# The last 3 of 39 expert blocks of a decoder kernel, put in a conditional block

## The chip, the cores and the metric

One core of one Trainium2 chip. The metric is the device time of one execution in microseconds, the median of three runs.

## The reference, cut to what matters

A decoder of two layers over 8 x 256 = 2048 tokens of width 512, in float32. Layer 0: differential attention, a long convolution with the context, then a mixture of 8 experts, of which each token takes two. Layer 1: self-attention, cross-attention, attention with one routed head. Each of the six parts ends in a residual sum and a layer norm. The expert part is what the change touches:

```python
logits = h @ router_w.T
probs = jax.nn.softmax(logits.astype(jnp.float32), axis=-1)
vals, idx = lax.top_k(probs, TOP_K)            # TOP_K = 2
vals = vals / vals.sum(axis=-1, keepdims=True)
combine = combine.at[jnp.arange(T)[:, None], idx].add(vals)
...
def step(acc, per_expert):
    gup, dp, cw = per_expert
    gate, up = jnp.split(h @ gup.T, 2, axis=-1)
    y = jax.nn.silu(gate) * up @ dp.T
    return (acc + cw[:, None].astype(acc.dtype) * y, None)
```

Two of 8 experts per token make 4096 pairs of a token and an expert. How many fall on which expert is known only when the logits are.

## The kernel before, in words

The stages run one after another on the core. The expert stage overlaps with the end of the convolution and stands directly ahead of self-attention.

**Sending tokens to experts.** `router` computes the logits in two halves of the tokens. Each token row, normalized, is written to `xd` (L761) and, by indirect DMAs on POOL (`send`, L825), to `xs` in DRAM, where every expert has a region of ROWS = 2176 rows; `slots` holds the row of each pair. The tokens of an expert lie there without gaps.

**The table of blocks.** Work is cut into blocks of 128 rows of one expert. `block_table` counts how many blocks each expert needs (`nb`), sums these up along the experts (`end`), and finds for each block number its expert (`i_ex`) and its first row (`i_row`). It runs twice: after the first half of the tokens it lists NE = 9 blocks that are already full; after the second half it lists the other NB - NE = 30. NB = 39 is the most that any routing can need (4096/128 + 7). Where fewer are needed, the remaining numbers get the last expert and rows without tokens, and are computed all the same.

**A block** (`blocks`, from L942) has these steps:
- `load` reads its expert number into a register of TensorE (L955) and its row into one of SP (L962), and SP loads its rows, `first_h<-xs` (L970), 256 KB, into one of four buffers, three blocks ahead;
- `turn` transposes the rows (pt, L188 and L217);
- `gate_up` makes the gate and up products pg and pu (L194), 8 matmuls, and silu on ScalarE and DVE (L1013 to L1015);
- `down` transposes the result (pt_m, L1023), copies it to hT (L1025, L1026), makes the down product po_m (L1032), copies it to y_m (L141 on DVE, L139 or L1041 on ScalarE), and SP stores it to `ys` at the same row (L1044). The row is in a register, so each store of `ys` waits for the one ahead.

For the 9 early blocks the order on TensorE, DVE and ScalarE is written out by hand, between token tiles of the second half. For the other 30, L1080 to L1088, a scheduler sets it by priorities; it lets four downs fall behind, which end the stage in two pairs. During block 18 `meanwhile` starts the loads of self-attention's weights.

**After the blocks.** `combine(t)` (L1090) loads x[t] from `xd` (SP, L1097), gathers the two expert rows of each token from `ys` (POOL, L1099, one indirect DMA per expert choice), and adds them with their weights (DVE, L1108). Layer norm follows: statistics on DVE (L168, L169), the inverse root on POOL (L163, L164), the normalization on DVE (L177). Self-attention works on groups of four tiles; its first group needs t = 0 to 3, and begins with transposes of x (pt, L217) and the products ps_f (L205).

Of the kernel before, what the change touches and what calls it, by code (L numbers as in the profile page):

```python
# [24 lines left out]
P = 128  # L25
B, S, D = 8, 256, 512
# [13 lines left out]
E, FF = 8, 352  # L40
FCH = [(0, 128), (128, 128), (256, 96)]
KPAD = 128 + D
NB = 2 * B * S // P + E - 1
ROWS = B * S + P
PH = NT // 2
NE = (PH * 2 * P - E * (P - 1) - 1) // P + 1
# [3 lines left out]
def decoder_kernel(ctx: ExitStack, tc: tile.TileContext, a: dict, out: bass.AP):  # L50
    nc = tc.nc
# [10 lines left out]
    rt = ctx.enter_context(tc.tile_pool(name="m_rt", bufs=1))  # L62
# [52 lines left out]
    xd = dram.tile([NT, P, D], F32, tag="xd", name="xd")  # L115
    xs = dram.tile([E * ROWS, D], F32, tag="xs", name="xs")
    ys = dram.tile([E * ROWS, D], F32, tag="ys", name="ys")
    ctx_d = dram.tile([P, KB, B * S], F32, tag="ctx_d", name="ctx_d")
# [16 lines left out]
    def evacuate(dst, src):  # L135

        flip[0] ^= 1
        if flip[0]:
            nc.scalar.copy(dst, src)  # L139
        else:  # L140
            nc.vector.tensor_copy(dst, src)  # L141
# [42 lines left out]
    def transpose(psum, dst, src):  # L184

        pt = psum.tile([P, KB, P], F32, tag="tr", name="pt")
        for k in range(KB):
            nc.tensor.transpose(pt[:, k, :], src[:, k * P : (k + 1) * P], ident)  # L188
        evacuate(dst, pt)
# [23 lines left out]
    def turned(pools, dst, src, tag="mm"):  # L213

        pt = pools.tile([P, KB, P], F32, tag=tag, name="pt")
        for k in range(KB):
            nc.tensor.transpose(pt[:, k, :], src[:, k * P : (k + 1) * P], ident)  # L217
        nc.scalar.copy(dst, pt)  # L218
# [436 lines left out]
    def experts(rt):  # L655
# [7 lines left out]
        tables = {}  # L663
# [30 lines left out]
        def clear_slots(pool):  # L694
# [3 lines left out]
            for e in range(E):  # L698
                for region in (xs, ys):
                    nc.sync.dma_start(  # L700
                        out=region[e * ROWS : (e + 1) * ROWS, :].rearrange(
                            "(p r) d -> p r d", p=P
                        ),
                        in_=zero.unsqueeze(1).broadcast_to([P, ROWS // P, D]),
                    )
# [6 lines left out]
        def router(work, rows_late):  # L712
# [15 lines left out]
                base,  # L728
                pattern=[[ROWS, E]],
                base=0,  # L730
# [123 lines left out]
        def block_table(ps_t, counts, half):  # L854
# [3 lines left out]
            def t8(name):  # L858
                return rt.tile([P, E], F32, tag=name, name=name)
# [4 lines left out]
            full = rt.tile([P, NT], F32, tag="full", name="full")  # L864
            blk = rt.tile([P, NB], F32, tag="blk", name="blk")
            for row, step in ((full, P), (blk, 1)):
# [23 lines left out]
            end = t8("end")  # L890
# [6 lines left out]
            nc.vector.tensor_tensor(first, end, nb, ALU.subtract)  # L897
            count = NB - NE if half else NE
            shape = [P, count, E]
            blk = blk[:, :count]  # L900
            bb = blk.unsqueeze(2).broadcast_to(shape)
            c = rt.tile([P, NB, E], F32, tag="c_b", name="c_b")[:, :count]
            nc.vector.tensor_tensor(c, end.unsqueeze(1).broadcast_to(shape), bb, ALU.is_le)
            ex = rt.tile([P, NB], F32, tag="ex", name="ex")[:, :count]
            nc.vector.tensor_reduce(ex, c, AX.X, ALU.add)
# [3 lines left out]
            nc.vector.tensor_tensor(c, c, first.unsqueeze(1).broadcast_to(shape), ALU.mult)  # L909
            row = rt.tile([P, NB], F32, tag="row", name="row_b")[:, :count]  # L910
            nc.vector.tensor_reduce(row, c, AX.X, ALU.max)
            nc.vector.tensor_tensor(row, blk, row, ALU.subtract)
            if half == 0:

                done = tables["done"] = t8("done")
                nc.vector.tensor_scalar(done, first, -1.0, float(NE), ALU.mult, ALU.add)
                nc.vector.tensor_scalar(done, done, 0.0, None, ALU.max)
                nc.vector.tensor_tensor(done, done, nb, ALU.min)
            else:

                nc.vector.scalar_tensor_tensor(
                    c,
                    idx.unsqueeze(1).broadcast_to(shape),
                    float(E),
                    ex.unsqueeze(2).broadcast_to(shape),
                    ALU.add,
                    ALU.is_equal,
                )
                nc.vector.tensor_tensor(
                    c, c, tables["done"].unsqueeze(1).broadcast_to(shape), ALU.mult  # L930
                )
                more = rt.tile([P, NB], F32, tag="more", name="more")[:, :count]
                nc.vector.tensor_reduce(more, c, AX.X, ALU.add)
                nc.vector.tensor_tensor(row, row, more, ALU.add)
            nc.vector.tensor_scalar(row, row, float(NT), float(P), ALU.min, ALU.mult)
            nc.vector.scalar_tensor_tensor(row, ex, float(ROWS), row, ALU.mult, ALU.add)
            for name, src in (("ex", ex), ("row", row)):
# [4 lines left out]
        def blocks(ps_t, buffers, late_tokens, meanwhile):  # L942


            with ExitStack() as st:
# [3 lines left out]
                xb, behind = {}, []  # L949
# [44 lines left out]
                def turn(b):  # L994
                    xT[b] = work.tile([P, KB, P], F32, tag="xT", name="xT_b")
                    if b < NE:
                        turned(ps_t, xT[b], xb[b][2], "tr")
                    else:
                        transpose(ps_t, xT[b], xb[b][2])

                def gate_up(b):
                    e, row, _ = xb.pop(b)
                    x_b = xT.pop(b)
                    pg = psum.tile([P, FF], F32, tag="g", name="pg")
                    pu = psum.tile([P, FF], F32, tag="u", name="pu")
                    for i, ps in enumerate((pg, pu)):
                        project(
                            ps,
                            lambda k: x_b[:, k, :],
                            lambda k: gu[k][i][:, bass.ds(e, 1), :],  # L1010
                        )
                    h = work.tile([P, FF], F32, tag="h", name="h_b", bufs=4)
                    nc.scalar.activation(h, pg, AF.Sigmoid)  # L1013
                    nc.vector.tensor_tensor(h, h, pg, ALU.mult)  # L1014
                    nc.vector.tensor_tensor(h, h, pu, ALU.mult)  # L1015
                    behind.append((b, e, row, h))

                def down(then=lambda: None):

                    b, e, row, h = behind.pop(0)  # L1020
                    pt = ps_t.tile([P, 3, P], F32, tag="tr", name="pt_m")
                    for i, (f0, m) in enumerate(FCH):
                        nc.tensor.transpose(pt[:m, i, :], h[:, f0 : f0 + m], ident)  # L1023
                    hT = work.tile([P, 3, P], F32, tag="hT", name="hT")
                    nc.scalar.copy(hT[:, 0:2, :], pt[:, 0:2, :])  # L1025
                    (nc.scalar.copy if b < NE else nc.vector.tensor_copy)(  # L1026
                        hT[:96, 2, :], pt[:96, 2, :]
                    )
                    then()
                    po = psum.tile([P, D], F32, tag="o", name="po_m")  # L1030
                    for i, (_, m) in enumerate(FCH):
                        nc.tensor.matmul(  # L1032
                            po,
                            lhsT=hT[:m, i, :],
                            rhs=dn[i][:m, bass.ds(e, 1), :],
                            start=(i == 0),
                            stop=(i == len(FCH) - 1),
                        )
                    y = work.tile([P, D], F32, tag="y", name="y_m")
                    if b < NE:  # L1040
                        nc.scalar.copy(y, po)  # L1041
                    else:
                        evacuate(y, po)
                    return nc.sync.dma_start(out=ys[bass.ds(row, P), :], in_=y).ins.name  # L1044
# [32 lines left out]
                        gate_up(b)  # L1077
                        down(lambda: turn(b + 1))
                load(NE + 2)
                for b in range(NE, NB):  # L1080
                    if b + 3 < NB:
                        load(b + 3)
                    gate_up(b)
                    stored = down(lambda: b + 1 < NB and turn(b + 1))
                    if b == NE + 9:
                        meanwhile(stored)
                while behind:
                    down()  # L1088

        def combine(t, buffers):  # L1090

# [21 lines left out]
            return load, add, lambda: norm[0]()  # L1113

        return clear_slots, load_experts, load_gu_last, router, blocks, combine, wide


# [578 lines left out]
    clear_slots, load_experts, load_gu_last, router, blocks, combine, wide = experts(rt)  # L1696
    diff_attention()
    with ExitStack() as st_self:


        half = B * P * KB
# [108 lines left out]
```

## Time and profile before

| what | value |
|---|---|
| median of three runs | 2341.53 us (2339.19 to 2346.2) |
| profiled execution, own time | 2344.37 us |
| its span | 2342.5 us |
| mean granted TensorE clock | 0.971 |
| expert blocks, first pg to last y_m | from 840.4 to 1195.7 us |
| first product ps_f of self-attention | 1223.41 us |
| one ys store, issue to landing, median | 2.0 us |
| one x<-xd load, issue to landing, median | 4.4 us |

All times in the text are microseconds from the start of the span of this profiled execution. PE is TensorE, DVE VectorE, ACT ScalarE, POOL GpSimd, SP the engine that issues most DMAs; PEld is TensorE's weight load, which overlaps its matmuls. A line such as L1032 is a line of the kernel before. In the chain of waits each piece has a start, a length and what ran or was waited for; it is followed back from the last instruction of the execution, so that what is not in it did not set the end. In a list by stretch, each engine has its busy time and, in brackets, its number of instructions.

### The profile page before, as it was taken

The page shows a single profiled execution, that of the slowest core. Times are in us where ns is not written, and L with a number is a line of the kernel's source. Part 1 is how long each engine was busy: PE and PEld are TensorE (multiplying, and loading weights), DVE is VectorE, ACT ScalarE, POOL GpSimd, SP SyncE. Part 2 cuts the span into 40 slices and gives each one's busy share as a digit, 9 for nine tenths or more (in the row PEclk, how much of TensorE's full clock was granted, in tenths as well). Part 3 has the DMA queues.
Part 4 walks back from the last instruction along what each step waited for, and adds up shares of the span by engine and source line. Part 5 has one row for each costly group of instructions (what it writes and reads, how often), then busy time and mean ns, then how long its engine had stood idle before and what let it go on. Part 6 is the DMA issues. An engine that isn't in the chain of part 4 may idle for free.

```text
span 2342.5 us, 35493 instructions
## 1 busy us (share of the span) xinstructions
PE 2170.8 (93%) x15151; PEld 1176.5 (50%) x15151; DVE 1202.4 (51%) x1858; ACT 428.9 (18%) x616; POOL 660.0 (28%) x768
## 2 busy tenths in 40 slices
PE   7799989879998998999959999998999999999996
PEld 4455555544453464555534454444545545555543
DVE  3566666657888962222224556452212213467767
ACT  1223233320010021111112222221101110122212
POOL 0344544456556622000022324230000000022223
PEclk9999999999999998999979999999999999999998
DMA  6899302306024143131140112003001000000000
GB/s 243 330 407 407 143 11 69 98 1 219 28 84 141 32 158 121 61 135 63 50 151 19 46 37 64 1 1 126 19 18 36 1 0 1 1 7 14 10 19 28
DMA packets 108715, 199.10 MB, mean 85 GB/s; under 512 B 7056, under 2 KB 26640, under 8 KB 108560
## 3 DMA queue, kind: packets, MB, share of 16 engines
q1 hardware_dynamic: 103440, 180.06, 21.7%
q0 software_dynamic: 5120, 16.78, 2.2%
q8 instruction: 121, 1.98, 0.3%
q14 instruction: 34, 0.28, 0.0%
HBM read 94.32 MB, written 112.98 MB: 88 GB/s over the span
## 4 chain that ended last, share of the span: by engine, by line
PE 72%; DVE 9%; POOL 8%; DMA 3%; ACT 3%; issue 2%; SPq 1%; another core or an unknown queue 0%; ACTq 0%; POOLq 0%; DVEq 0%
PE ps_y L194 9%; PE ps_f L205 8%; PE ps_t L205 7%; PE ps_f L194 5%; PE po_m L1032 5%; PE pg L194 4%; PE ps_o L205 4%; PE pu L194 4%; PE ps_k L1235 3%; PE ps_q L1181 3%; PE ps_t L194 2%; PE po_x L194 2%; PE ps_o L194 2%; PE ps_pv L1288 2%; POOL pT L1263 2%; POOL pT L1253 2%
## 5 line engine op out<-in xcount | busy, mean ns | idle before, releaser
L1188 DVE TENSOR_REDUCE neg<-ps_q 128x12 f32<-128x1536 f32 x128 | 224.9, 1757 | 342.5 <-PE ps_q L1181 341.7
L194 PE MATMUL ps_y<-kv,wt 128*128 128x512 f32 x640 | 282.4, 600 | 5.7 <-POOL kv L562 3.8
L1253 POOL TENSOR_SCALAR_AFFINE_SELECT pT<-pT 128x1024 f32<-128x1024 f32 x128 | 140.3, 1097 | 513.2 <-ACT pT L1252 443.4
L1252 ACT ACTIVATE pT<-ps_k 128x1536 f32<-128x1536 f32 x128 | 185.8, 1452 | 537.4 <-PE ps_k L1244 515.6
L1296 DVE RECIPROCAL rsum<-ps_pv 128x256 f32<-128x256 f32 x128 | 224.1, 1751 | 40.5 <-PE ps_pv L1288 39.7
L194 PEld LDWEIGHTS ps_y<-kv,wt 128*128 128x128 f32 x640 | 120.9, 192 | 155.7 <-issue 137.0
L163 POOL TENSOR_SCALAR rstd<-bn_mv 128x1 f32<-128x1 f32 x80 | 17.0, 213 | 560.5 <-DVE bn_mv L169 556.5
L1263 POOL TENSOR_TENSOR pT<-pT 128x512 f32<-128x512 f32 x112 | 142.4, 1271 | 9.4
L1032 PE MATMUL po_m<-dn,hT 128*128 (+1 forms) x234 | 113.0, 621 | 12.0 <-ACT hT L1025 10.5
L194 PE MATMUL ps_f<-xT,w_l1x 128*128 128x512 f32 x256 | 120.7, 615 | 3.3 <-ACT qT L1460 2.1
L205 PE MATMUL ps_f<-xT,w_l1a 128*128 128x512 f32 x256 | 119.7, 611 | 3.0 <-ACT xT L218 3.0
L205 PE MATMUL ps_t<-w_l1f,xT 128*128 128x512 f32 x256 | 120.1, 607 | 0.3 <-DVE sel L1627 0.3
L1099 POOL DMA_INDIRECT w_l1x<-ys,slots x32 | 32.6, 1018 | 307.6 <-DMA ys<-y_m 299.7
L1288 PE MATMUL ps_pv<-pT,ones_v 128*32 128x256 f32 (+1 forms) x1152 | 86.0, 381 | 12.7 <-POOL pT L1263 10.6
L600 DVE TENSOR_REDUCE yc<-z 128x64 f32<-128x512 f32 x128 | 86.1, 674 | 6.2 <-POOL w_l1a L601 5.8
L1171 PEld LDWEIGHTS <-ident_b 128*128 128x128 bf16 x512 | 50.4, 99 | 75.4 <-issue 71.6
L1171 PE MATMUL ps_q<-hide_b,ident_b 128*128 128x256 bf16 x512 | 77.7, 275 | 9.7 <-ACT pT L1252 8.7
L194 PE MATMUL pg<-gu,xT_b 128*128 x234 | 77.9, 469 | 1.4 <-ACT xT_b L218 1.4
L194 PEld LDWEIGHTS ps_f<-xT,w_l1x 128*128 128x128 f32 x256 | 47.0, 194 | 62.7 <-issue 47.6
L1235 PE MATMUL ps_k<-qT,kz 32*128 32x256 f32 (+1 forms) x1024 | 69.5, 358 | 8.4 <-DVE neg L1188 6.7
L205 PEld LDWEIGHTS ps_f<-xT,w_l1a 128*128 128x128 f32 x256 | 46.9, 192 | 59.1 <-issue 54.3
L1014 DVE TENSOR_TENSOR h_b<-h_b,pg 128x352 f32<-128x352 f32 x39 | 20.3, 521 | 108.1 <-ACT h_b L1013 108.1
(303 smaller groups left out, 3545.7 us busy)
## 6 DMA issues: line engine op xcount, KB each, us to landing
xs<-zero SPq DMA_DIRECT2D x8, 4352.0 KB, 31.2
ys<-zero SPq DMA_DIRECT2D x8, 4352.0 KB, 28.0
filters<-in_L_xattn_k SPq DMA_DIRECT2D x4, 2560.0 KB
first_h<-xs SPq DMA_DIRECT2D x39, 256.0 KB, 2.6
ys<-y_m SPq DMA_DIRECT2D x39, 256.0 KB, 2.0
gu<-in_L_ffn_gate_up_proj SPq DMA_DIRECT2D x3, 2816.0 KB, 19.1
wt<-filters SPq DMA_DIRECT2D x32, 256.0 KB, 2.6
x<-in_x SPq DMA_DIRECT2D x16, 256.0 KB, 5.0
```

What stands on the lines that cost most here:

```text
L194: nc.tensor.matmul(ps, lhsT=lhsT(k), rhs=rhs(k), start=(k == 0), stop=(k == n - 1))
L205: nc.tensor.matmul(ps[0], lhsT=lhsT(k), rhs=rhs(k), start=(k == 0), stop=(k == KB - 1))
L600: nc.vector.tensor_reduce(yc[:, lb], z, AX.X, ALU.add)
L1032: nc.tensor.matmul(po, lhsT=hT[:m, i, :], rhs=dn[i][:m, bass.ds(e, 1), :], start=(i == 0), stop=(i == len(FCH) - 1),)
L1171: nc.tensor.matmul(block[:, s, 0:3:2, :], lhsT=ident_b, rhs=hide_b.unsqueeze(1).broadcast_to([P, 2, P]), start=True, stop=False,)
L1188: nc.vector.tensor_reduce(neg[(u // upb) % 2][:, :, :, c].rearrange("p j s -> p s j"), block, AX.X, ALU.max, negate=True,)
L1235: nc.tensor.matmul(block[:, s, at, :], lhsT=k(rows, c, b * S + j * P, P), rhs=q(rows, c, b * S + j * P, P * (2 - j)), start=True, stop=False,)
L1252: nc.scalar.activation(p[:, 0:3].rearrange("p j s q -> p s j q"), block, AF.Exp)
L1253: nc.gpsimd.affine_select(out=p[:, 0:2].rearrange("p j s q -> p (j s) q"), in_=p[:, 0:2].rearrange("p j s q -> p (j s) q"), compare_op=ALU ...
L1263: nc.gpsimd.tensor_tensor(p[:, 3], p[:, 1], p[:, 2], ALU.add)
L1288: nc.tensor.matmul(ps[32 * s : 32 * s + 32, 1, j * P :], lhsT=ones_v, rhs=p[:, 1, s, :] if j else first[:, :, s, :], start=(j == 0), stop= ...
L1296: nc.vector.reciprocal(r, ps[:, 1, :])
```

## The change

`block_table` keeps the total of its second run as an integer. The loop over the late blocks ends at NS = 36 instead of NB = 39, with all pending downs behind it. Then the total is read into a register on every engine, and blocks 36 to 38 stand in a conditional block, which an engine enters if more than NS - NE = 27 late blocks are needed. Inside, the three loads come first, and the downs stay one block behind.

```diff
 NB = 2 * B * S // P + E - 1
+NS = 2 * B * S // P + E // 2
...
             nc.vector.tensor_tensor(row, blk, row, ALU.subtract)
+            if half == 1:
+                tables["count"] = rt.tile([P, 1], mybir.dt.int32, tag="i_count", name="i_count")
+                nc.vector.tensor_copy(tables["count"], end[:, E - 1 : E])
             if half == 0:
...
                 load(NE + 2)
-                for b in range(NE, NB):
-                    if b + 3 < NB:
+                for b in range(NE, NS):
+                    if b + 3 < NS:
                         load(b + 3)
                     gate_up(b)
-                    stored = down(lambda: b + 1 < NB and turn(b + 1))
+                    stored = down(lambda: b + 1 < NS and turn(b + 1))
                     if b == NE + 9:
                         meanwhile(stored)
                 while behind:
                     down()
+
+                count = nc.values_load(
+                    tables["count"][0:1, 0:1],
+                    min_val=0,
+                    max_val=NB - NE,
+                    skip_runtime_bounds_check_because="a count of blocks",
+                )
+                assert NB - NS <= len(buffers)
+                with tc.If(count > NS - NE):
+                    for b in range(NS, NB):
+                        load(b)
+                    for b in range(NS, NB):
+                        turn(b)
+                        gate_up(b)
+                        if len(behind) > 1:
+                            down()
+                    while behind:
+                        down()
```

## The prediction

> **What bounds the kernel now.** I read the page's totals first, then the chain of waits around the expert blocks, then the tail of that stage piece by piece, then busy time by stretch.
>
> ```profile
> span 2342.5 us, 35493 instructions
> ...
> PE 2170.8 (93%) x15151; PEld 1176.5 (50%) x15151; DVE 1202.4 (51%) x1858; ACT 428.9 (18%) x616; POOL 660.0 (28%) x768
> ```
>
> TensorE is busy 93% of the span, so removing TensorE work can pay, if the stage it stands in is bound by TensorE. The chain of waits, stretch 1150 to 1226 us (start, length, what), says that the expert blocks are:
>
> ```profile
> 1166.59 2.85 PE po_m L1032 x6
> 1169.44 2.37 PE pg L194 x8
> 1171.81 2.37 PE pu L194 x8
> 1174.17 0.33 PE pt_m L1023 x3
> 1174.50 0.44 PE pt L188 x4
> 1174.94 0.03 issue
> 1174.96 2.84 PE po_m L1032 x6
> ```
>
> From one po_m to the next is 1174.96 - 1166.59 = 8.37 us, all of it TensorE but 0.03 us: that is the price of a block. The same view at the end of the stage:
>
> ```profile
> 1188.75 0.67 PE pt_m L1023 x6
> ...
> 1190.07 3.15 DMA ys<-y_m
> ...
> 1193.33 3.38 DMA ys<-y_m
> ...
> 1196.83 3.07 DMA ys<-y_m
> 1199.89 0.02 issue
> ...
> 1200.75 1.00 POOL w_l1x L1099
> ...
> 1218.37 0.59 POOL rstd L164
> ...
> 1219.58 3.17 PE pt L217 x12
> ```
>
> After the last product the chain runs through the stores of ys, one after another, and then through POOL: its gathers of ys rows (1.0 us each and 0.3 us between) and the rstd steps queued among them, until TensorE gets the tokens of self-attention. So TensorE already stands empty between the stages, and everything of self-attention starts from the last landing of ys, at 1199.89. Call that moment L. The same stage by stretch (busy us of each engine, then granted clock, DMA share, GB/s):
>
> ```profile
> 1183.20:1195.00 11.80, 11.50 (x30) 5.10 (x30) 1.84 (x5) 2.28 (x6) 0.00 (x0) 1.00 0.95 321
> 1195.00:1200.00 5.00, 0.00 (x0) 0.00 (x0) 0.69 (x1) 0.00 (x0) 0.00 (x0) 0.97 0.87 283
> 1200.00:1223.40 23.40, 4.24 (x16) 2.86 (x16) 11.18 (x23) 2.35 (x4) 16.50 (x20) 0.50 0.48 135
> ```
>
> The reader is to see that DMA is nearly full (0.95) under the last products: there the 16 loads x<-xd run, 4.2 MB. After L it is half empty, and POOL is the busy engine.
>
> [...]
>
> **Whether the block is entered.** I counted the tokens of each expert with the reference on its own inputs: 505, 488, 479, 474, 539, 531, 555, 525. In blocks of 128 that is 4+4+4+4+5+5+5+5 = 36. The first half supplies 9 of them, the counter then holds 27, and 27 > 27 is false: all three blocks are skipped. The nearest upset is an expert going from 505 to 513.
>
> **The change part by part.** The instructions of each engine in order, before against after, show: the same tail of two pairs of down products now ends with block 35; then on every engine a register load and a compare-and-branch; behind the body a waiting branch for the path that skips it; nothing else differs on TensorE, DVE, ScalarE and POOL, and SP's loads x<-xd all stand behind the conditional.
>
> 1. Three blocks removed: 3 x 8.37 = -25.1 us, on the path. The last y_m, which ends at 1195.70 now, ends at 1170.6. (Blocks 36 to 38 hold no token; their cost before was full all the same.)
> 2. Stores without x loads beside them. The ys stores wait for one another. A store lands in 2.0 us at the median, in 3.1 in this tail, and the last was issued 1.1 us after its data (1196.83 against 1195.70) because the one ahead had not landed. With x loads gone from there: -1.1 - 1.1 = -2.2 us. Bounds: 0 (something else held it) and -2.3. I take -2.2. L moves from 1199.9 to about 1172.6.
> 3. The conditional on the path. SP passes its waiting branch when all ys stores have landed, and the gathers on POOL wait for the semaphores that SP then raises. Some seven semaphore steps (17 ns each in SP's rows)[...] I take +0.5. Register loads: 0.27 us on SP and 0.30 on TensorE by the rows of i_row and i_ex; SP's lies under the 2 us that the last store takes to land. TensorE, DVE and ScalarE pass while they stand idle (20.4 us, 3.6 us and 23.5 us before their next step). POOL passes near 905 us, 300 us early.[...] Lower bound 0, as nothing here can gain.
> 4. Loads moved. What is queued behind SP's wait is all 16 loads x<-xd (0.33 to 0.46 us each to issue), and DVE's first add (L1108) waits for them. x0 is issued at L + 0.5 instead of 18 us before it (1181.98). A load landed in 3.3 to 4.6 us; 4 loads are 1.05 MB, 3.3 us at 321 GB/s, so x0 is there by L + 4 and x3 by L + 6, or twice the transfer time beside gathers: L + 9. Needed: x0 with the first gather at L + 4.2, x3 at L + 12.6 (DVE at 1204.09 and 1212.48). The gathers in turn share with the loads: 8 gathers of 0.26 MB at half of 321 GB/s take 13 us, so the eighth lands near L + 16 instead of L + 14. POOL covers that: rstd of tile 0 has its input at 1207.8 and is computed at 1211.44 (3.6 us of slack), the last of the group is due at L + 20.1, and two microseconds behind L + 14.0 plus 2.4 us of DVE work are still ahead of it. Cost 0 if the cover holds; +3.4 us if the loads go first entirely (12 us for 4.2 MB would put the eighth gather at L + 21.6, its statistics at L + 23.5 against L + 20.1). I take +1.0.
> 5. DVE's copy into i_count: 0.17 us by the row of a copy of 128x8 in the same function, hidden by the 6.4 us DVE idles at 897 before its next step; 0.17 us if not.
>
> Sum: -25.1 - 2.2 + 0.5 + 1.0 + 0 = -25.8 us. The profiled execution took 2344.37 us with a span of 2342.5 (1.9 us around it); it would become 2318.6. It stands 2.8 us above the median of the three runs, 2341.53, against which the same sum gives 2315.7: I say 2316.
>
> **The rivals.**
> A, the forecast: skipped, POOL still sets the start of self-attention: 2316, own range 2310 to 2320.
> B, skipped, but the moved loads become the wait:[...] the loads start late and crowd out the gathers. For it: SP has no cover, and the x loads alone filled 0.95 of DMA. Against: slack of 2 to 4 us at every rstd. Price: +3.4 from step 4[...]. Then 2316 - 1 + 6.4, about 2322.
> C, on the other side: the body is entered, because the kernel counts 37 or more. The place is the end of the stage: the pipeline is drained, then filled again. TensorE ends at 1169.9, SP issues the loads near 1171.3, the rows land (2.6 us) at 1174.3; transpose and copy 1.3, two blocks of pg and pu 9.5, one turn and po_m 3.6, pg and pu 4.7, the last pairs 6.5, copy and store 3.0: L is 1202.9, 3.0 later than now; plus 1.5 for steps 3 and 4, plus 3.5 for 7 us at half clock after the gap: +8.0, 2349.5. It decides from 37 blocks on. Against: the count of 36, eight tokens from the limit.
>
> **How the numbers follow.** A 0.70, B 0.20, C 0.08, others 0.02. The range 2310 to 2328 holds most of A and B (about 0.85) and the spread of 7 us that three runs of before show. About 0.3%, 7 us, is what a measurement of this kernel can tell from no change. Faster by more than that: A and B, 0.90. C lies at the limit and is halved: same 0.05, slower 0.05.
>
> **What would show it.** In the profile after: 36 blocks, so po_m x216 instead of x234; the last y_m near 1170.6 and the last ys landing near 1172.6; the store's landing back at 2.0 us; x<-xd all behind it; the first gather within 1.5 us of it; from L to the first ps_f of self-attention 23.5 us as now (more than 26 us is B). po_m x234 and a gap on TensorE before the last three blocks would be C. The prediction is wrong if the stores' serial wait stays, or if a stall of over 10 us stands behind the branch on SP, DVE or TensorE.

## The result, and the profile after

The changed kernel took 2318.39 us, median of four runs (2314.65 to 2321.55), against 2343.86 us for the kernel before, median of four (2339.19 to 2349.18): ratio 0.989, 95% interval 0.9862 to 0.9918, or 25.5 us less. The profiled execution of the changed kernel took 2321.55 us, the slowest of its four, with a span of 2319.8 us.

Lines of the changed kernel carry other numbers than those of before: po_m is L1036, the stores of ys L1048, the loads x<-xd L1119, the gathers L1121, the adds L1130, the conditional L1101, its register load L1094. First its page (totals, then the group of the down products):

```profile
span 2319.8 us, 35250 instructions
...
PE 2148.9 (93%) x15064; PEld 1164.0 (50%) x15064; DVE 1194.6 (51%) x1847; ACT 424.1 (18%) x607; POOL 658.8 (28%) x768
...
L1036 PE MATMUL po_m<-dn,hT 128*128 (+1 forms) x216 | 104.5, 622 | 11.8 <-ACT hT L1029 10.3
```

216 products are 36 blocks of 6: the conditional was skipped. TensorE is busy 21.9 us less, about as much as the span is shorter (22.7 us in this pair of profiles). The timeline of DVE and then of SP around the end of the stage (start, length, what, and in brackets how long it was idle before and what it waited for):

```profile
1172.64 0.69 DVE L142 COPY y_m<-po_m 128x512 f32<-128x512 f32 x1 [4.87 <-PE po_m L1036]
...
1181.97 0.75 DVE L1130 SCALAR_TENSOR_TENSOR x<-w_l1x,v,x 128x512 f32<-128x512 f32 x1 [5.80 <-DMA w_l1x<-ys,slots]
...
1191.91 0.73 DVE L1130 SCALAR_TENSOR_TENSOR x<-w_l1x,v,x 128x512 f32<-128x512 f32 x1
```

```profile
1156.20 17.49 SPq L1048 DMA_DIRECT2D ys<-y_m  x5
1175.21 13.06 SPq L1119 DMA_DIRECT2D x<-xd  x16
```

The last y_m ends at 1173.33, the 16 loads all follow the stores. (The prediction had 1170.6 for this end. The stage as a whole began 3.0 us later in this execution: its first pg is at 843.4, where before had 840.4.) The same steps of DVE in the kernel before, the last y_m, then the first and the eighth add:

```profile
1195.01 0.69 DVE L141 COPY y_m<-po_m 128x512 f32<-128x512 f32 x1 [4.86 <-PE po_m L1032]
...
1204.09 0.75 DVE L1108 SCALAR_TENSOR_TENSOR x<-w_l1x,v,x 128x512 f32<-128x512 f32 x1 [3.59 <-DMA w_l1x<-ys,slots]
...
1213.93 0.75 DVE L1108 SCALAR_TENSOR_TENSOR x<-w_l1x,v,x 128x512 f32<-128x512 f32 x1
```

And the chain of waits from there to self-attention:

```profile
1173.36 2.01 DMA ys<-y_m
...
1176.23 1.00 POOL w_l1x L1121
...
1178.80 7.22 DMA w_l1x<-ys,slots
...
1186.98 0.19 POOL rstd L164
...
1195.27 3.17 PE pt L218 x12
...
1199.10 6.24 PE ps_f L206 x10
```

Two things differ from the chain of before. There is one store of ys in it instead of three, and it lands in 2.01 us. And between POOL's gathers now stands a landing, w_l1x<-ys,slots, with 7.22 us: the gathers that come first have become slow enough to be seen. (In the second trace of this same kernel, **again** below, the chain runs through POOL's gathers all the way, as before: ahead of the first rstd step POOL is idle for 0.74 us there and for 0.77 us here, which the trace gives to no releaser there and to DVE here.) The stage by stretch, from the last landing of ys to the first ps_f (length, busy us of PE, PEld, DVE, ACT and POOL, granted clock, DMA share, GB/s):

```profile
1175.40:1199.10 23.70, 4.25 (x17) 2.87 (x17) 11.02 (x23) 2.34 (x4) 16.01 (x20) 0.50 0.86 310
```

DMA is busy 0.86 of it with 310 GB/s, where it was 0.48 with 135 before; POOL's busy time is nearly the same (16.0 against 16.5 us), and so is the length (23.7 against 23.4). The loads have moved into a stretch that had room for them.

In what follows, Y is the end of the last y_m, L the last landing of ys, F the first ps_f of self-attention.

### The profile page after: what moved, and what is told of

It reads as the page before. It is cut to its first block, busy times and chain, and to the rows that moved or that the text cites. A ratio compares the mean times of both kernels' runs of the same rounds, so it can differ in the third digit from the quotient of the medians.

```text
span 2319.8 us, 35250 instructions
## 1 busy us (share of the span) xinstructions
PE 2148.9 (93%) x15064; PEld 1164.0 (50%) x15064; DVE 1194.6 (51%) x1847; ACT 424.1 (18%) x607; POOL 658.8 (28%) x768
## 4 chain that ended last, share of the span: by engine, by line
PE 40%; DVE 5%; POOL 2%; ACT 1%; issue 1%; DMA 1%; POOLq 0%; ACTq 0%; DVEq 0%
PE ps_f L206 7%; PE ps_t L206 6%; PE ps_f L195 5%; PE ps_t L195 2%; PE po_x L195 2%; PE ps_o L206 2%; PE ps_o L195 2%; PE ps_q L1203 2%; PE ps_x L195 2%; PE ps_k L1257 2%; PE ps_pv L1300 2%; PE ps_pv L1310 1%; DVE rsum L1318 1%; DVE neg L1210 1%; DVE bn_st L169 1%; PE ps_q L1193 1%
## 5 line engine op out<-in xcount | busy, mean ns | idle before, releaser
L1036 PE MATMUL po_m<-dn,hT 128*128 (+1 forms) x216 | 104.5, 622 | 11.8 <-ACT hT L1029 10.3
L1121 POOL DMA_INDIRECT w_l1x<-ys,slots x32 | 32.3, 1011 | 280.1 <-DMA ys<-y_m 272.3
L195 PE MATMUL pg<-gu,xT_b 128*128 x216 | 72.1, 470 | 1.4 <-ACT xT_b L219 1.4
```

The source lines that it names most:

```text
L195: nc.tensor.matmul(ps, lhsT=lhsT(k), rhs=rhs(k), start=(k == 0), stop=(k == n - 1))
L1036: nc.tensor.matmul(po, lhsT=hT[:m, i, :], rhs=dn[i][:m, bass.ds(e, 1), :], start=(i == 0), stop=(i == len(FCH) - 1),)
```

## The experiments

Theory 1 is that of the prediction: the blocks are worth what TensorE spends on them, the stores land sooner without loads beside them, and what the conditional adds is covered. Theory 2: the conditional costs several microseconds that the gain of the blocks hides. Two sets of four kernels, again to entered and x_late to cond_end; the kernel before had a median of 2342.88 us in the first set and 2341.63 us in the second. The row "changed" is the result above, with its ratio to 2343.86 us. if_only and cond_end turned out to hold no branch, as told below. The fourth column is from the first y_m copied by DVE (block 9) to Y; columns 4 to 7 are read in the timeline and the chain of each kernel's profile.

| kernel | median us | ratio (95%) | late blocks | Y to L | L to first add | L to F |
|---|---|---|---|---|---|---|
| before | 2342.88 | 1 | 227.1 | 4.2 | 4.2 | 23.5 |
| changed | 2318.39 | 0.989 (0.9862 to 0.9918) | 202.0 | 2.1 | 6.6 | 23.7 |
| again | 2319.85 | 0.9903 (0.9887 to 0.9919) | 202.0 | 2.1 | 6.8 | 24.1 |
| no_if | 2318.77 | 0.9896 (0.9878 to 0.9913) | 202.0 | 4.3 | 4.1 | 23.0 |
| if_only | 2344.12 | 1.0002 (0.9992 to 1.0012) | 227.2 | 2.0 | 6.5 | 23.8 |
| entered | 2353.75 | 1.0041 (1.0025 to 1.0056) | 235.2 | 2.2 | 7.3 | 24.5 |
| x_late | 2314.77 | 0.9888 (0.9867 to 0.991) | 202.0 | 2.1 | 5.7 | 23.3 |
| order | 2312.73 | 0.9877 (0.9857 to 0.9898) | 202.0 | 2.1 | 6.1 | 22.7 |
| both | 2310.71 | 0.9858 (0.9836 to 0.9879) | 202.0 | 2.0 | 5.8 | 20.7 |
| cond_end | 2345.09 | 1.0012 (1.0002 to 1.0023) | 227.2 | 3.6 | 4.1 | 22.9 |

**again**: the changed kernel, unedited.

> The changed kernel once more, as the reference for the other runs of this set. Theory 1 (three TensorE-bound blocks go, the stores land sooner, what the conditional adds is covered): 25 to 27 us below the kernel before, ratio about 0.989. Theory 2 (the conditional costs 5 us or more that the removed blocks hide): the same ratio; this run doesn't tell them apart. In the trace both expect the last y_m to end 2.0 us ahead of the last landing of ys, and 23.7 us from there to the first ps_f of self-attention.

It came 23.0 us below the kernel before, a little short of the expected 25 to 27, with the expected times in the trace (2.1 us from Y to L; 24.1 us from L to F instead of 23.7). Both theories allow it.

**no_if**: the three blocks left out, no conditional.

```diff
                 while behind:
                     down()
-
-                count = nc.values_load(...)
-                with tc.If(count > NS - NE):
-                    ...
```

> Blocks 36 to 38 are left out altogether, without a conditional (with these inputs they hold no token). Theory 1: the blocks alone are worth 3 x 8.37 = 25.1 us, and SP's x<-xd loads go back among the last stores, so the last ys lands about 4.2 us after the last y_m ends, and first ps_f follows 23.5 us later: 25.1 us below the kernel before, some 2 us slower than the changed kernel. Theory 2: without the cost of the conditional this is at least 5 us faster than the changed kernel, 30 us or more below the kernel before.

24.1 us below the kernel before, and as fast as the changed kernel within the intervals. Theory 2 wanted 30 us or more; the interval ends at 28.6. Theory 2 falls here. Its chain shows what the conditional had moved:

```profile
1162.57 3.30 DMA ys<-y_m
...
1165.98 3.82 DMA ys<-y_m
...
1169.92 2.58 DMA ys<-y_m
```

The loads stand among the stores again, three stores are in the chain, and the last lands 4.3 us after Y, as it did before. The sum from block 9 to F is 229.3 us, against 227.8 and 228.2 with the conditional and 254.8 before. So by the trace the version with the conditional is ahead by 1 to 1.5 us of the one without. The medians have it 1.1 us behind (again against no_if), and their intervals overlap; they can't resolve it.

**if_only**: all 39 blocks, then what was meant as a conditional that is never entered.

```diff
-NS = 2 * B * S // P + E // 2
+NS = NB
...
                 with tc.If(count > NS - NE):
-                    for b in range(NS, NB):
+                    for b in range(NB - 1, NB):
                         load(b)
-                    for b in range(NS, NB):
+                    for b in range(NB - 1, NB):
```

> All 39 blocks stand ahead of the conditional, which is never entered (more than 39 blocks can't be needed). Nothing is saved, only the register loads, the branches, the waits of the skipping path and the moved x<-xd loads are added. Theory 1: the stores land 2.2 us sooner, and join and contention take 0.2 us: 2 us faster than the kernel before, within its spread; last y_m to last landing 2.0 us instead of 4.2, landing to first ps_f 23.7 us. Theory 2: 3 to 5 us slower than the kernel before, with a gap behind the branch.

The edit did not make the kernel that it was meant to make. The count is declared with a maximum of NB - NE = 30, and the condition became count > 30, which that bound rules out. Its trace has no compare-and-branch on any engine, and nothing reads i_count. Of the conditional only a boundary is left, with a few semaphore steps, and the loads x<-xd stand behind it. All that the trace has of i_count, and the store of ys in its chain:

```profile
L916 DVE CAST i_count<-end x1: 146/146/146, 898.9 to 898.9; 128x1 int32<-128x1 f32 x1
...
1200.17 2.02 DMA ys<-y_m
```

So its time can't say what register loads and branches cost. It shows the moved loads alone: the last store lands 2.0 us after Y, as in the changed kernel, and block 9 to F takes 252.9 us instead of 254.8, 1.9 us less. The whole is 1.0002 of before (0.9992 to 1.0012, so between 1.9 us less and 2.8 us more). As a second reference it does price the register loads and branches within the stage: the changed kernel, which has them, needs 2.1 us from Y to L against 2.0 here, and 23.7 and 24.1 us from L to F against 23.8.

**entered**: the threshold lowered by one, so that the conditional is entered.

```diff
-                with tc.If(count > NS - NE):
+                with tc.If(count > NS - NE - 1):
```

> The threshold is lowered by one, so the 27 counted late blocks enter the conditional, and all 39 blocks run, 36 to 38 behind the branch. Theory 1 by the prediction's case C: the pipeline is drained and filled again, last landing of ys 3 us later than in the kernel before, join and contention 1.5 us, half clock after the gap 3.5 us: 8 us slower than the kernel before, ratio 1.0034. Theory 2: with 5 us for the conditional on top, 13 us slower. If drain and refill cost less than the estimate: 0 to 4 us slower.

Slower by a ratio of 1.0041 (1.0025 to 1.0056), 9.6 us; from block 9 to F its trace has 261.8 us against 254.8, 7.0 more. The changed kernel skips at a count of up to 27 and this one enters from 27 on, so the two put the count of late blocks at exactly 27. TensorE's timeline shows the drain:

```profile
1168.59 5.42 PE L1036 MATMUL po_m<-dn,hT 128*128 x12
1179.10 1.09 PE L189 MATMUL pt<-ident,first_h 128*128 128x128 f32 x4 [5.09 <-DMA first_h<-xs]
```

TensorE stands for 5.09 us until rows that only the body may load have landed; the transposes behind it take 1.09 us where they take 0.60 in the steady blocks. The granted clock is 0.86 in the mean from 1173 to 1181 and 0.98 from 1181 to 1208. As an estimate from these two, taking all that is missing from 1 as time at 0.50, it is at half from about 1179 to 1182. Case C of the prediction is what happens where an input needs a 37th block.

**x_late**: the loads of tiles 4 to 15 wait for the gathers of tile 3.

```diff
-                nc.sync.dma_start(out=x[t], in_=xd[t])
+                row = nc.sync.dma_start(out=x[t], in_=xd[t])
+                if t >= TPG:
+                    wait_for(row.ins, gathered[-1], "not among the first group's gathers")
...
+                if t < TPG:
+                    gathered.append(got.ins.name)
```

> The changed kernel, with x<-xd loads of tiles 4 to 15 held back until the gathers of tile 3 have landed, so that the first group's gathers share DMA with 4 loads instead of 16. Theory 1 (POOL's order of gathers and rstd steps sets the start of self-attention, the moved loads are covered by slack): the first gathers land earlier, the first add about 4.5 us after the last landing of ys instead of 6.6, but the first ps_f still comes 23.2 to 23.7 us after it, and the time is that of the changed kernel within 0.5 us. Rival B (the moved loads are the wait): first ps_f 2 to 3 us earlier.

The first add came 5.7 us after L, earlier than 6.6 but later than expected, and F after 23.3 us, 0.4 us sooner than in the changed kernel and 0.8 us sooner than in again. Rival B wanted 2 to 3. Twelve of the 16 loads taken away give back less than a microsecond: with POOL's order as it is, the loads are covered.

**order**: POOL's gathers from tile 4 on behind the first group's rstd steps; of these, tiles 4 and 5 had stood among them.

```diff
+                    if t >= TPG:
+                        wait_for(got.ins, roots[TPG - 1], "behind the first group's norms")
...
+                roots[t] = root[-1]
```

> The changed kernel, with POOL's four gathers of tiles 4 and 5 placed behind the first group's rstd steps instead of among them; the loads stay as they are. Theory 1: POOL no longer stands between, what is left is the landing of the gathers beside the 16 loads (eighth gather about 16.5 us after the last ys) and DVE behind it: first ps_f after 21.3 us instead of 23.7, 2.4 us less. Rival (POOL's queue isn't what the start waits for): no change from 23.7.

F after 22.7 us: 1.0 us less instead of 2.4. POOL's order was in the way, but the next wait stood close behind it.

**both**: the two edits together.

> Both edits together: loads of tiles 4 to 15 held back and the later gathers behind the first group's rstd steps. Theory 1: the eighth gather lands about 13 us after the last ys, and nothing of POOL stands between: first ps_f after 18 to 19 us, 5 us less than in the changed kernel, so about 30 us below the kernel before. If only one of the two were a limit, this would equal the better of the two single edits.

F after 20.7 us, 3.0 us less; I had expected 5. The two don't equal the better of the single edits (22.7), so both were limits, one behind the other: with POOL's order out of the way, the twelve loads cost 2.0 us (22.7 against 20.7). Its chain names what is left:

```profile
1185.01 3.79 DMA w_l1x<-ys,slots
...
1188.90 0.75 DVE x L1142
1189.65 0.09 DVE bn_mv L172
1189.74 0.44 DVE x L180
1190.18 0.14 issue
1190.32 3.94 PE pt L220 x16
...
1194.91 1.13 PE ps_f L208 x2
```

The eighth gather's own landing comes 14.6 us after L, where 13 was expected. Behind it stand DVE and 16 transposes in one row, 3.94 us, where the chain of the changed kernel has 12 of them in 3.17 us. This kernel is 30.9 us below the kernel before and the fastest of those tried. Its interval (0.9836 to 0.9879) lies just below that of the changed kernel in **again**, but overlaps that of the result. Of the distance of some 9 us from again, the stage has only 3.4. The rest lies outside it; the granted clock, 0.9720 against 0.9690 in the mean, can account for some 4 us by the estimate under cond_end.

**cond_end**: the kernel before, with what was meant as a conditional that is never entered at its very end. In the first six profiles the four taken to hold a conditional had been 2 to 4 us later in the first 23 us of the program.

```diff
         routed_attention(*w_routed)
+    count = nc.values_load(counted[0][0:1, 0:1], ...)
+    with tc.If(count > NB - NE):
+        nc.vector.memset(counted[0], 0)
```

> The kernel before, with all 39 blocks as they were, and only a conditional that is never entered (a memset in it) at the very end of the program. It asks whether a program that holds a conditional is later from its start: in the four kernels with one, the first score product ps_q of the first attention came at 22.5 to 24.3 us, in the two without at 20.4 and 20.8. Theory 3 (it belongs to having a conditional): ps_q at 22.5 us or later, and 2 to 3 us slower than the kernel before. Theory 1 (it is chance from run to run): ps_q anywhere from 20 to 24 us, and within 1 us of the kernel before.

This condition, count > 30, is ruled out in the same way, and the trace again holds neither a read of i_count nor a compare-and-branch. So cond_end holds no conditional, and theory 3 is not tested by it. The ten traces answer its first half all the same. The first ps_q in TensorE's timeline of cond_end, of if_only and of x_late, of which only x_late branches:

```profile
20.27 0.60 PE L1175 MATMUL ps_q<-hide_b,ident_b 128*128 128x256 bf16 x4
```

```profile
23.47 0.60 PE L1193 MATMUL ps_q<-hide_b,ident_b 128*128 128x256 bf16 x4
```

```profile
19.98 0.60 PE L1199 MATMUL ps_q<-hide_b,ident_b 128*128 128x256 bf16 x4
```

(The times in the expectation are those of the products that follow this row by 0.9 us.) The four kernels without a branch start at 19.51 (before), 19.99 (no_if), 20.27 and 23.47 us, the six with one between 19.98 and 22.61. The latest start of all belongs to a kernel without a branch, so a late start is not the mark of a conditional.

cond_end was nevertheless slower by 1.0012 (1.0002 to 1.0023), 0.5 to 5.4 us. A likely reason is the granted clock of each execution, which goes along with its time: the kernel before in this set took 2337.9 us at a clock of 0.972 and 2348.47 us at 0.966, and over its 19 executions a straight line has about 1.4 us less for each 0.001 more. By that estimate the mean clock of cond_end, 0.9688 against 0.9703, is worth 2.1 us of the difference. Why an execution gets one clock or another is not shown.

## Why the prediction was right, point by point

- **Entered or not**: 36 blocks counted from the reference's inputs, 36 computed. Right.
- **Step 1, the blocks, -25.1**: 227.1 to 202.0 is 25.1 us in every kernel that leaves three blocks out. Right, because the chain had nothing but TensorE in a block.
- **Step 2, the stores, -2.2**: from Y to L 4.2 before, 2.1 after: 2.1 us. no_if, in which the loads are back among the stores, has 4.3 again, and if_only, with all blocks and no branch, has 2.0: the moved loads alone do it. (With the loads among the stores it is 3.6 to 4.3 us in three profiles, with the loads behind them 2.0 to 2.2 in seven.) Right.
- **Step 3, the join, +0.5**: nothing of it is seen on the path. Of the 0.5, seven semaphore steps of 17 ns are 0.12; the rest was the author's estimate for two branches. SP's compare-and-branch took 0.05 us. The prediction let SP pass only when all stores of ys had landed, so that its steps and the first load came behind L. They did not. Rows of the register load and of the conditional in the changed kernel (length in ns, first start in us):

```profile
L1094 PEldq TENSOR_LOAD <-i_count x1: 594/594/594, 1167.9 to 1167.9; - x1
...
L1094 DVEq TENSOR_LOAD <-i_count x1: 545/545/545, 1172.7 to 1172.7; - x1
L1094 SPq TENSOR_LOAD <-i_count x1: 274/274/274, 1173.7 to 1173.7; - x1
```

```profile
L1101 SPq EVENT_SEMAPHORE  x7: 17/17/17, 1174.2 to 1175.1; - x7
...
L1101 PEldq COMPARE_BRANCH  x1: 397/397/397, 1168.6 to 1168.6; - x1
...
L1101 DVEq COMPARE_BRANCH  x1: 72/72/72, 1173.3 to 1173.3; - x1
...
L1101 SPq COMPARE_BRANCH  x1: 50/50/50, 1174.1 to 1174.1; - x1
```

  SP's seven semaphore steps lie before L (1175.37), its first load goes out at 1175.21, 0.16 us before L instead of 0.5 after it, and POOL's first gather starts 0.86 us behind L as it did before. Against if_only, which has neither register load nor branch, Y to L differs by 0.1 us and L to F by -0.1 and +0.3. The register load was under-priced on TensorE and DVE (0.3 us taken from the row of i_ex; 0.59 and 0.55 measured), which cost nothing as both stand idle there (20.72 us before TensorE's next step, 2.52 us before DVE's).
- **Step 4, the loads, +1.0**: L to F grew by 0.2 us (changed) and 0.6 us (again), against no_if by 0.7 and 1.1; cond_end, with the loads among the stores, has 22.9, so the growth is 0.2 to 1.2. The path to it was as worked out: the first add went from L + 4.2 to L + 6.6, the eighth from L + 14.0 to L + 16.5 (L + 16 said), and POOL's slack took it. That the gathers get half of the DMA rate beside the loads was an assumption of the author's estimate: from 1175.2 to 1191.9 they moved 2.10 of 5.48 MB, and the loads 3.37. The slack is used up, though: POOL's first rstd step waits 0.77 us for DVE in the changed kernel, where it waited for nothing. x_late says that these loads cost 0.4 to 0.8 us behind POOL's order. The upper bound of +3.4 was too low by its own numbers: 4.2 MB take 13.1 us at the 321 GB/s of the same step, not 12, which makes it 4.5.

```profile
1186.98 0.19 POOL L164 TENSOR_SCALAR rstd<-bn_mv 128x1 f32<-128x1 f32 x1 [0.77 <-DVE bn_mv L170]
```

- **Step 5, the copy into i_count**: it took 0.15 us, and no run isolates what it costs. The distance from the first pg to block 9 is 124.0 to 128.1 us in the nine profiles with the copy and 128.2 us in that of before, the only one without it, so no cost of it can be seen.
- **The sum, -25.8**: the stage from block 9 to F gained 27.0 us, by 25.1 + 2.1 - 0.2. The medians show 25.5 and 23.0, and the interval of the first of them goes from 19.2 to 32.3. That -25.8 meets -25.5 within 0.3 us is luck: the stage gained 1.2 us more than the sum, and 1.5 us were lost outside it (in again 3.6: 26.6 in the stage, 23.0 in all), which the sum has no term for. The profiles differ there from run to run: the first pg comes between 840.4 and 847.9 us in the ten of them, and from F to the end they need 1114 to 1121 us. The granted clock takes up part of it. again ran at a mean of 0.9690 against 0.9704 for the kernel before, by the estimate above 2.0 us, so that 23.0 becomes 25.0; no_if, with 24.1, ran at 0.9704. Whether a conditional costs a microsecond or two outside the stage stays open: if_only and cond_end hold none, and the intervals of again and no_if, 1.1 us apart by their medians, are each 7 to 8 us wide.
- **Rival B** had its mechanism right (crowded gathers) and its price wrong: no stall stands behind SP's branch (50 ns, and the first semaphore step follows within 0.1 us), and the slack held. The 3 us of its price that are not from step 4 were the author's estimate for such a stall, sized by DVE's 6.43 us of idle time up to 903.41 in the kernel before, of which 3 to 4 were taken as slack; no run shows one.
- **Rival C**, +8.0: entered measured +9.6 (5.9 to 13.1), 7.0 in the stage. L moved by 6.0 us (3.0 for the refill and 3.5 for half clock had been said), L to F by 1.0 (1.5 said). (The 7 us at half clock fit the kernel before: its granted clock is 0.50 until 1227.0, 7.4 us past the start of the row of transposes at 1219.58.) The granted clock, 0.9683 against 0.9704 in the mean, takes 2.9 of the 9.6 by the estimate above. The two terms of the 6.0 missed in opposite ways: the clock was at 0.50 for about 3 us by the estimate under entered and not 7, which is some 1.5 us lost by estimate, so that about 4.5 are left for the refill. (Its sum also has the rows landing at 1174.3, where 1171.3 + 2.6 gives 1173.9.)

## What to carry to other kernels

Work that some inputs don't need can be skipped at run time at a cost that did not show here, where the engines already stand between two stages, and the price of the skipped work was its start-to-start distance on TensorE, the engine that bounds it: 8.37 us a block, 25.1 us for three. Look also at what can no longer be interleaved across the conditional: here loads were pushed out of a full DMA stretch (0.95 busy) into a half-empty one (0.48), which helped the stores (2.1 us) and was paid by slack that is now gone. The limit belongs to the input: one block more than the threshold turned 25 us of gain into 7 to 10 us of loss, so the choice of 36 needs the distribution of the counts. And look in the trace for what a control kernel is meant to hold: two of these had lost their branch, and their times alone did not tell.

## What the runs showed of the hardware that was not expected

- In the changed kernel a compare-and-branch took 45 to 72 ns on POOL, ScalarE, SP and DVE and 397 ns on TensorE; in entered, TensorE's two took 90 and 188 ns. Why TensorE's skip took longer is not shown.
- Loading the count into a register cost 0.27 us on SP and 0.46 to 0.59 us on the other four engines.
- With 16 loads on SP's queue and POOL's gathers at once, DMA gave 310 GB/s and the first gather's add came 2.4 us later. Both moved on together: the first gather's rows were added at 1181.97, while SP issued loads until 1188.27, and from 1175.2 to 1191.9 the loads' queue moved 3.37 MB and the gathers' queue 2.10 MB.
- A mean granted clock that was higher by 0.001 went with about 1.4 us less in 2342 us (19 executions of the kernel before, 0.966 to 0.972). A difference of 2 us between two medians can be no more than that.
